# A pair's two state stores joined into one, and one gather tile in 128 fetched row by row by SyncE

## The chip, the cores and the metric

The kernel runs on one core of a Trainium2 chip. The metric is device time in microseconds. A core has TensorE (PE) for matrix products, VectorE (DVE), ScalarE (ACT) and GpSimd (POOL), each with its own instruction queue, and SyncE (SP), which here does nothing but issue transfers and wait. SyncE and GpSimd both issue transfers (DMAs), and these run on the same 16 DMA engines.

## The reference

A graph layer: 12500 nodes of 128 features, 400000 edges sorted by destination, 8 heads of 16 channels (C).

```python
h   = relu(layernorm(x))
hn  = layernorm(h) * ln1_g + ln1_b
x_l, x_r = hn @ W_l, hn @ W_r                       # per node
# every edge, and one self loop a node with the mean edge_attr
m     = leaky_relu(x_l[src] + x_r[dst] + edge_attr @ W_e, 0.2)
alpha = sum over channels of m * att                # one score per edge and head
a     = softmax of alpha over the edges of each dst
out   = segment_sum(x_l[src] * a, dst) + bias
h     = h + out
y     = x + h + gelu(layernorm(h) @ W1 + b1) @ W2 + b2
```

So every edge needs the x_l row of its source, which is anywhere in memory, and every destination needs a softmax and a sum over some 32 neighbouring edges.

## The kernel before

**Units and pairs.** The sorted edges are cut into units of 256 (U). Two units make a pair (UP), of four tiles of 128 edges; there are 3125 tiles and 782 pairs. A unit holds about 8 destinations, and the kernel gives it a window of 16 nodes (NW): for each of these 16 x 8 node-heads it collects the lowest score, the sum of weights and the weighted sum of rows, 18 numbers (SH, 72 bytes) in each of 128 partitions. This record is stored to memory at the window's place, and the final stage reads the records back by node. Since windows of neighbouring units overlap, there are two state tensors: even units write to the first, odd ones to the second. A later window of the same tensor may overwrite only what the earlier one did not use, so the stores to one tensor must land in order; their addresses come from registers, and each store waits until the one before it to its tensor has landed. A test on the device, `fits`, checks from the destinations that all windows hold their units; if not, a slower general path runs.

**Before the main loop** the node features are normalised tile by tile (`node_stages`, rounds of four tiles), the x_l rows (136 numbers, 544 bytes) are stored to `xl_dram`, and the destinations are turned into differences (`from_first`, `as_float`, `differ`) and into the addresses of windows (`edge_constants`, L369 and L370). GpSimd meanwhile gathers raw rows of x for 29 pairs ("raw" pairs): their x_l is computed later from them, so they need no gather in the main loop.

**The main loop** is written out by hand: rounds r from -4 on, and in each round every stage runs for the pair that is due (`stages`, L1538 to L1562). The order of that text is the order of each engine's queue. Pair c is gathered in round c-4 (`gather`, L955, GpSimd, one indirect transfer a tile, with 128 row numbers each), placed by DVE at the end of round c-1 (`place`, L995), multiplied on TensorE in round c (`combine`, L1009 and L1012), then scored, weighed, and collected in round c+6 (`collect`, L1072). In round c+7 DVE takes each node's own heads (`own_heads`, L1081 and L1087) and SyncE stores the record (`put`, L1098). A pair's gathered rows `xs` stand in one of 12 buffers, which is free again after `collect`.

**SyncE's queue in a round**, in order: rows of a raw pair if one is due (L950); in every second of the first 196 rounds 512 KB of edge attributes for their mean (`sum_load`, L1107); in every eighth round up to 104 two stores that clear a part of the state (`clear`, L728); loads and stores of the final stage (L1151 to L1159, L1401) and of the row tables (L632 to L719); in every fourth round the four loads of the next four pairs (`windows`, three rounds ahead: ea, dl, du, then a register load L938 and zw); last the two stores of `put`, with a register load of eight addresses in every fourth round. SyncE stops at the first instruction whose condition is not met, and all behind it waits.

```python
stages = ((-AHEAD, gather), (LATE + 1, own_heads), (5, keep_turned), (0, combine), ...
          (3, weigh), (-1, place))
late_stages = ((-WAHEAD, windows), (LATE + 1, put))
AHEAD, LATE, WAHEAD, QP = 4, 6, 3, 4
rows = es.enter_context(tc.tile_pool(name="e_rows", bufs=AHEAD + LATE + 2))
```

Of the kernel before, what the change touches and what calls it, by code (L numbers as in the profile page):

```python
# [13 lines left out]
F32 = mybir.dt.float32  # L14
# [8 lines left out]
P = 128  # L23
# [21 lines left out]
PW = OR * OS  # L45
CW = UP * NW
WN = P - DE
# [15 lines left out]
LEAD = 2  # L63
KEPT = 7
BIG = 2.0**126
CAP = 2.0**120
# [77 lines left out]
def tile_gnn(  # L144
# [55 lines left out]
    first_sb = keep.tile([1, NU], I32, name="first_sb")  # L200
    win_sb = keep.tile([1, NU // QU], I32, name="win_sb")
    flag = keep.tile([1, 1], I32, name="flag")
    quads = [(t, min(GN, NT - t)) for t in range(0, NT, GN)]
# [47 lines left out]
    def load_consts():  # L251
# [9 lines left out]
        nc.sync.dma_start(b2_r, row_bcast(b2, P))  # L261
        nc.sync.dma_start(first_sb, bass.AP(tensor=dst.tensor, offset=dst.offset, ap=[[0, 1], [U, NU]]))
# [102 lines left out]
    def edge_constants():  # L365
        of = build.tile([P, H], F32, name="of")
        mine = build.tile([P, H], F32, name="mine")
        below = build.tile([P, P // NW], F32, name="below")
        nc.vector.tensor_scalar(win_sb, first_sb[:, 0:NU:QU], float(P * 4), None, op0=OP.mult)  # L369
        nc.vector.tensor_scalar(first_sb, first_sb, float(H * SH * 4), None, op0=OP.mult)  # L370
        nc.vector.tensor_copy(
# [28 lines left out]
    bad = rng.tile([RP, PARTS + 1], F32, name="bad")  # L400
    junk = rng.tile([RP, EP], BF16, name="junk")
    nf = rng.tile([RP, RU], F32, name="nf")
    dlb = rng.tile([RP, EP], BF16, name="dlb")
    dlr = rng.tile([RP, RU // UP, OR, OS], BF16, name="dlr")
# [10 lines left out]
    def from_first():  # L415
        nc.vector.tensor_copy(nf, dc[:, 0:EP:U])
        nc.vector.memset(dlr[:, :, :, OW:OS], 0.0)
        nc.vector.tensor_scalar(nf, nf, -1.0, None, op0=OP.mult)

# [11 lines left out]
    def differ(i):  # L431
        for u in range(UP * i, UP * i + UP):
            es = slice(u * U, (u + 1) * U)
            nc.scalar.activation(dlb[:, es], df[:, es], AF.Identity, bias=nf[:, u : u + 1])
        e = UP * U * i
        nc.scalar.activation(
            dlr[:, i, :, 0:OW], df[:, e : e + OR * OW].rearrange("p (a b) -> p a b", b=OW), AF.Identity,
            bias=nf[:, i // QP * QU : i // QP * QU + 1],
        )
# [7 lines left out]
    def fits():  # L447

        fu = rng.tile([RP, RU + 2], F32, name="fu")
        lf = rng.tile([RP, RU], F32, name="lf")  # L450
        real = rng.tile([RP, RU], F32, name="real")
        off = rng.tile([RP, 4, RU], F32, name="off")
# [3 lines left out]
        nc.vector.tensor_copy(fu, df[:, 0 : (RU + 1) * U + 1 : U])  # L456
        nc.vector.tensor_copy(lf, lu)

        nc.vector.tensor_sub(off[:, 0], lf, fu[:, 0:RU])
        nc.vector.tensor_sub(  # L460
# [3 lines left out]
        )  # L464
        nc.vector.tensor_tensor(off[:, 2], lf, fu[:, 2 : RU + 2], op=OP.is_ge)
        nc.vector.tensor_scalar(real, lf, float(NO_NODE // 2), None, op0=OP.is_lt)
# [9 lines left out]
        nc.vector.tensor_scalar(off[:, 3], place, float(SPARE**2), None, op0=OP.is_gt)  # L476
        nc.vector.tensor_mul(off, off, real[:, None, :].to_broadcast([RP, 4, RU]))
        nc.vector.tensor_reduce(bad[:, PARTS : PARTS + 1], off.rearrange("p k u -> p (k u)"), AX.X, OP.max)
# [272 lines left out]
    with tc.manual_schedule():  # L751
# [15 lines left out]
        for r in range(max(max(len(qs), 9) + LAST + 1, 16 + PARTS, rows_at[-1] + KEPT + 1)):  # L767
# [11 lines left out]
            if r == 14:  # L779
                nc.sync.dma_start(src_sb, src)  # L780
            if r == 10:
                from_first()
# [26 lines left out]
    with tc.If(fast == 1) as cmp:  # L809
        window_edges(  # L810
            tc, n_edges, ea_t, NT, NE, NUE, ident, wer, weh, negrep, diag, nid, farw, bias_r, b2_r, w1_sb, w2_sb,
            cols, xl_dram, xl_t, xr_dram, xr_t, dc_dram, du_dram, late_dram, state, clear, xr_steps, qs, raw_steps, raw, x_t, out_t, h_sb, src_sb, first_sb, win_sb, wid,
        )
# [67 lines left out]
def window_edges(  # L881
    tc, n_edges, ea_t, NT, NE, NUE, ident, wer, weh, negrep, diag, nid, farw, bias_r, b2_r, w1_sb, w2_sb,
    cols, xl_dram, xl_t, xr_dram, xr_t, dc_dram, du_dram, late_dram, state, clear, xr_steps, qs, raw_steps, raw, x_t, out_t, h_sb, src_sb, first_sb, win_sb, wid,
):
# [27 lines left out]
    with ExitStack() as es:  # L912
# [30 lines left out]
        def rows_at(t, at, n, size):  # L943

            return t.rearrange("n f -> (n f)").bitcast(U8)[ds(at, n * size)].rearrange("(n f) -> n f", f=size)

        def gather(c):
            xs = rows.tile([P, KP, XW], F32, name="xs")
# [4 lines left out]
            for t in tiles_of(c):  # L953
                for j in t:
                    nc.gpsimd.indirect_dma_start(  # L955
                        out=xs[:, j, :],
# [47 lines left out]
        def combine(c):  # L1004
# [3 lines left out]
            for j in range(e // P):  # L1008
                nc.tensor.matmul(  # L1009
                    z[:, j * P : (j + 1) * P], d["xs"][:, j, 0:P], ident, start=(j == 0), stop=False, is_transpose=True  # L1010
                )
# [53 lines left out]
        def collect(c):  # L1065
# [4 lines left out]
            for i, js in enumerate(tiles_of(c)):  # L1070
                for j in js:
                    nc.tensor.matmul(  # L1072
                        d["acc"][:, i, :], d["pt"][:, j * P : (j + 1) * P], d["xs"][:, j, :],
                        start=(j == js[0]), stop=(j == js[-1]),
                    )
# [15 lines left out]
        def put(c):  # L1091
            if c % QP == 0:
                at = words(first_sb[0:1, UP * c : UP * (c + QP)], (NT * P - CW) * H * SH * 4)
                for i in range(c, min(c + QP, n_pr)):
                    pairs[i]["put"] = at[UP * (i - c) : UP * (i - c + 1)]
            for i in range(len(tiles_of(c))):
                u = UP * c + i
                nc.sync.dma_start(  # L1098
                    rows_at(state[u % 2], pairs[c]["put"][i], NW * H, SH * 4), pairs[c]["rec"][:, i, :].bitcast(U8)
                )  # L1100

# [814 lines left out]
```

## Time and profile before

| | |
|---|---|
| median of three runs | 3963.11 us (3962.49 to 3964.65) |
| the profiled execution | 3958.53 us, span 3956.7 us |
| mean granted TensorE clock | 0.943 |
| PE busy | 3459.6 us (87%), 18462 instructions |
| POOL busy | 2957.3 us (75%), 3138 instructions |
| DVE busy | 2794.0 us (71%) |
| ACT busy | 2172.3 us (55%) |
| SyncE's transfers | 490760 packets, 330.85 MB, 35.7% of 16 DMA engines |
| GpSimd's transfers | 100000 packets, 217.32 MB, 31.1% |

How to read it: L12 is a line of the kernel. A group's row names line, engine, operation, output<-input and count, then the busy time and the mean of one in ns, then the engine's idle time just before and what ended it. In the rows of one line the three numbers are the shortest, median and longest duration in ns, followed by when the first and the last one start. A wait's row gives who waited, for whom, microseconds in total, how often, and the longest. In a timeline a row is start, length, engine, line and count; several instructions may be merged into one row. A window's row gives its stretch, its length, the busy time of PE, PE's weight loads, DVE, ACT and POOL with their counts, the granted clock, the share of time in which the DMA engines were busy, and GB/s. "q" behind an engine means its queue: SyncE shows only in this form.

### The profile page before, as it was taken

The page shows a single profiled execution, that of the slowest core. Times are in us where ns is not written, and L with a number is a line of the kernel's source. Part 1 is how long each engine was busy: PE and PEld are TensorE (multiplying, and loading weights), DVE is VectorE, ACT ScalarE, POOL GpSimd, SP SyncE. Part 2 cuts the span into 40 slices and gives each one's busy share as a digit, 9 for nine tenths or more (in the row PEclk, how much of TensorE's full clock was granted, in tenths as well). Part 3 has the DMA queues.
Part 4 walks back from the last instruction along what each step waited for, and adds up shares of the span by engine and source line. Part 5 has one row for each costly group of instructions (what it writes and reads, how often), then busy time and mean ns, then how long its engine had stood idle before and what let it go on. Part 6 is the DMA issues. An engine that isn't in the chain of part 4 may idle for free.

```text
span 3956.7 us, 60318 instructions
## 1 busy us (share of the span) xinstructions
PE 3459.6 (87%) x18462; PEld 2360.4 (60%) x18463; DVE 2794.0 (71%) x6131; ACT 2172.3 (55%) x4747; POOL 2957.3 (75%) x3138
## 2 busy tenths in 40 slices
PE   4589888898898899989889899898998998999888
PEld 3356565666566566666666666666665665666565
DVE  6477777877777777677767776677767666667665
ACT  7445555555565555555555555555555455455454
POOL 7777777777777777777777777777777777777774
PEclk6799999999999999999999999999999999999999
DMA  8788888777766666666666666666666665666663
GB/s 227 206 189 196 191 198 193 176 178 174 164 127 125 127 122 123 127 122 117 118 123 129 122 122 128 122 123 122 114 124 129 125 123 108 119 123 113 120 119 75
DMA packets 591812, 552.26 MB, mean 140 GB/s; under 512 B 299169, under 2 KB 469762, under 8 KB 591058
## 3 DMA queue, kind: packets, MB, share of 16 engines
q1 hardware_dynamic: 490760, 330.85, 35.7%
q0 software_dynamic: 100000, 217.32, 31.1%
q8 instruction: 150, 2.46, 0.3%
q14 instruction: 182, 1.49, 0.1%
q10 hardware_dynamic: 720, 0.13, 0.0%
HBM read 482.05 MB, written 65.88 MB: 138 GB/s over the span
## 4 chain that ended last, share of the span: by engine, by line
PE 40%; DMA 24%; POOL 20%; issue 11%; ACT 2%; DVE 2%; SPq 1%; POOLq 0%; DVEq 0%
DMA xs<-xl_dram,src_sb 22%; POOL xs L955 19%; PE z L1012 9%; PE acc L1072 9%; PE ab L1033 7%; PE pt_ps L1058 5%; PE z L1009 4%; PE ab L1018 2%; PE acc L1356 1%; PE acc L1381 1%; ACT h_sb L532 1%; SPq L308 1%; ACT sq L557 0%; DVE rec L1039 0%; PE pt_ps L700 0%
## 5 line engine op out<-in xcount | busy, mean ns | idle before, releaser
L955 POOL DMA_INDIRECT xs<-xl_dram,src_sb x3009 | 2842.2, 945 | 917.0 <-issue 794.8
L1050 ACT ACTIVATE p<-ab,rec 128x256 f32<-128x256 f32 x1563 | 656.3, 471 | 982.8 <-DVE rec L1039 974.2
L1081 DVE TENSOR_TENSOR own<-acc,diag 128x272 f32<-128x272 f32 x782 | 341.9, 437 | 845.3 <-PE acc L1072 837.4
L1009 PE MATMUL z<-ident,xs 128*128 128x128 f32 x3125 | 562.2, 283 | 383.1 <-DMA xs<-xl_dram,src_sb 343.5
L1072 PE MATMUL acc<-xs,pt 128*128 128x136 f32 x6250 | 892.1, 288 | 0.0
L1012 PE MATMUL z<-ea,zw 128*128 128x512 f32 x1564 | 854.4, 630 | 17.2 <-DMA zw<-xr_dram 10.8
L1009 PEld LDWEIGHTS z<-ident,xs 128*128 128x128 f32 x3125 | 398.9, 142 | 785.1 <-DMA xs<-xl_dram,src_sb 438.4
L1072 PEld LDWEIGHTS acc<-xs,pt 128*128 128x128 f32 x6250 | 821.3, 199 | 0.0
L1033 PE MATMUL ab<-m,negrep 128*128 128x512 f32 x1564 | 805.0, 596 | 0.0
L1063 ACT COPY pt<-pt_ps 128x512 f32<-128x512 f32 x782 | 455.6, 583 | 614.2 <-PE pt_ps L1058 606.0
L1058 PEld LDWEIGHTS pt_ps<-ident,p 128*128 128x128 f32 x3125 | 416.9, 149 | 361.3 <-issue 288.8
L1028 DVE TENSOR_TENSOR m<-z,zs 128x512 f32<-128x512 f32 x782 | 532.8, 681 | 128.0 <-ACT zs L1023 126.9
L995 DVE TENSOR_SCALAR ea<-dl,wid 96x516 f32<-96x516 bf16 x782 | 575.6, 736 | 24.3 <-DMA dl<-dc_dram 24.3
L1039 DVE TENSOR_REDUCE rec<-ab 128x2 f32<-128x512 f32 x781 | 538.4, 689 | 12.3 <-PE ab L1033 11.7
L1058 PE MATMUL pt_ps<-ident,p 128*128 128x128 f32 x3125 | 500.6, 286 | 1.7 <-ACT pt L1063 1.0
L1023 ACT ACTIVATE zs<-z 128x512 f32<-128x512 f32 x782 | 472.2, 604 | 43.9 <-DMA xs<-xl_dram,src_sb 37.5
L1087 DVE TENSOR_REDUCE rec<-own 128x34 f32<-128x272 f32 x782 | 340.8, 436 | 26.7
L1018 PE MATMUL ab<-ne,farw 128*128 128x512 bf16 x782 | 314.2, 402 | 20.0 <-ACT p L1050 18.8
L1012 PEld LDWEIGHTS z<-ea,zw 128*128 128x128 f32 x1564 | 257.6, 206 | 20.2 <-DVE ne L1002 10.8
L1033 PEld LDWEIGHTS ab<-m,negrep 128*128 128x128 f32 x1564 | 245.7, 195 | 1.1 <-DMA ea_s<-in_ea_t 0.7
L1018 PEld LDWEIGHTS <-farw 128*128 128x128 bf16 x782 | 79.6, 102 | 215.5 <-issue 110.5
L1050 ACT ACT_TABLE_LOAD x104 | 133.4, 1283 | 1.8
(232 smaller groups left out, 2168.3 us busy)
## 6 DMA issues: line engine op xcount, KB each, us to landing
dl<-dc_dram SPq DMA_DIRECT2D x196, 396.0 KB
ea<-in_ea_t SPq DMA_DIRECT2D x196, 256.0 KB
ea_s<-in_ea_t SPq DMA_DIRECT2D x98, 512.0 KB
xs<-xl_dram,src_sb POOLq DMA_INDIRECT x3009
state<-rec SPq DMA_DIRECT2D x1563, 9.0 KB
state<-empty SPq DMA_DIRECT2D x28, 504.0 KB
f_st<-state SPq DMA_DIRECT2D x46, 288.0 KB
du<-du_dram SPq DMA_DIRECT2D x196, 64.0 KB
```

The costliest lines, as they stand in the source:

```text
L955: nc.gpsimd.indirect_dma_start(out=xs[:, j, :], out_offset=None, in_=xl_dram, in_offset=bass.IndirectOffsetOnAxis(ap=src_sb[:, c * KP + j ...
L995: nc.vector.tensor_scalar(d["ea"][0:WN].rearrange("p (a b) -> p a b", b=OW), d["dl"][0:WN].rearrange("p (a b) -> p a b", b=OS)[:, :, 0:OW] ...
L1009: nc.tensor.matmul(z[:, j * P : (j + 1) * P], d["xs"][:, j, 0:P], ident, start=(j == 0), stop=False, is_transpose=True)
L1012: nc.tensor.matmul(z[:, :e], d["zw"], d["ea"][:, :e], start=False, stop=True)
L1018: nc.tensor.matmul(d["ab"][:, :e], d["far"], d["ne"][:, :e], start=True, stop=False)
L1023: nc.scalar.activation(d["zs"][:, :e], d["z"][:, :e], AF.Copy, scale=SLOPE)
L1028: nc.vector.tensor_tensor(d["m"][:, :e], d["z"][:, :e], d["zs"][:, :e], op=OP.max)
L1033: nc.tensor.matmul(d["ab"][:, :e], negrep.rearrange("p n h -> p (n h)"), d["m"][:, :e], start=False, stop=True)
L1039: nc.vector.tensor_reduce(d["rec"][:, :, CX], d["ab"].rearrange("p (u e) -> p u e", e=U), AX.X, OP.min)
L1050: nc.scalar.activation(d["p"][:, us], d["ab"][:, us], AF.Exp, bias=d["rec"][:, i, CX:SH], scale=-1.0)
L1058: nc.tensor.transpose(d["pt_ps"][:, js], d["p"][:, js], ident)
L1072: nc.tensor.matmul(d["acc"][:, i, :], d["pt"][:, j * P : (j + 1) * P], d["xs"][:, j, :], start=(j == js[0]), stop=(j == js[-1]),)
```

## The change

**One store for a pair.** The two states become slices of one tensor `state_dram`, with a spacing such that the windows of both units of a pair lie at a fixed distance. A pair now has one base, the smaller of (first destination of unit 0) + 12 and (first destination of unit 1). Unit 0's window starts at base - 12 (BEFORE), unit 1's at base - 3 (AFTER). One transfer with an address pattern of 128 partitions x 2 units x 72 bytes stores both records; `put` reads four addresses instead of eight in every fourth round. The starts used for the differences and for the test of windows are those of the new windows, computed on DVE before the main loop; the test has one more condition.

**Rows fetched by SyncE.** For some pairs (`hand_pairs`) GpSimd doesn't gather the last tile. Starting in round 8, and again every 32 rounds, SyncE fetches the 128 x_l rows of one such tile one by one, four (HR) in each of 32 rounds, into a tile of its own (two buffers), at the very beginning of the round. The pair is used 33 rounds after its first row (one more if it would be a raw pair). The row addresses are prepared before the main loop: 24 small loads of row numbers, one a handed tile, in round 14 behind the load of all row numbers, and one DVE multiply by the row's size in round 16. In the main loop SyncE reads 16 addresses into registers in every fourth round. `combine` and `collect` take these rows from the new tile (`row_of`).

```diff
+HR = 4
+HAND_AT = 8
+HAND_LEAD = 1
+def hand_pairs(nt, n_edges):
+    late = {c for c, _ in raw_pairs(nt, n_edges)}
+    n_full = n_edges // (UP * U)
+    hands, r = [], HAND_AT
+    while True:
+        c = r + P // HR + HAND_LEAD
+        while c in late:
+            c += 1
+        if c >= n_full:
+            return hands
+        hands.append({"c": c, "i": len(hands), "round": r})
+        r += P // HR
...
-    state = [dram.tile([NT * P * H, SH], F32, name=f"state{i}") for i in range(2)]
+    SR = (BEFORE + NT * P + NW) * H
+    state_dram = dram.tile([NT * P * H + 2 * (SR + (BEFORE - AFTER) * H), SH], F32, name="state")
+    state = [state_dram[i * SR + BEFORE * H : i * SR + (BEFORE + NT * P) * H] for i in range(2)]
...
-        nc.vector.tensor_scalar(first_sb, first_sb, float(H * SH * 4), None, op0=OP.mult)
+        nc.vector.tensor_scalar(first_sb, first_sb, float(BEFORE), None, op0=OP.add)
+        nc.vector.tensor_tensor(base_sb, base_sb, first_sb, op=OP.min)
+        nc.vector.tensor_scalar(base_sb, base_sb, float(H * SH * 4), None, op0=OP.mult)
...
             if r == 14:
                 nc.sync.dma_start(src_sb, src)
+                for d in hands:
+                    at = src.offset + (d["c"] + 1) * UP * KU - 1
+                    nc.sync.dma_start(
+                        hand_sb[d["i"] : d["i"] + 1, :],
+                        bass.AP(tensor=src.tensor, offset=at, ap=[[0, 1], [NCH * K, P]]),
+                    )
+            if r == 16:
+                nc.vector.tensor_scalar(hand_sb, hand_sb, float(XW * 4), None, op0=OP.mult)
...
+        def hand(r):
+            for d in hands:
+                k = r - d["round"]
+                if not 0 <= k < P // HR:
+                    continue
+                if k == 0:
+                    d["x"] = once.tile([P, XW], F32, name=f"hand{d['i'] % 2}")
+                if k % QP == 0:
+                    d["at"] = words(hand_sb[d["i"] : d["i"] + 1, k * HR : (k + QP) * HR], (NT * P - 1) * XW * 4)
+                for i in range(k * HR, (k + 1) * HR):
+                    nc.sync.dma_start(d["x"][i : i + 1, :].bitcast(U8), rows_at(xl_dram, d["at"][i - k // QP * QP * HR], 1, XW * 4))
...
             for t in tiles_of(c):
                 for j in t:
+                    if c in of_hand and j == KP - 1:
+                        continue
                     nc.gpsimd.indirect_dma_start(
...
         def put(c):
             if c % QP == 0:
-                at = words(first_sb[0:1, UP * c : UP * (c + QP)], (NT * P - CW) * H * SH * 4)
+                at = words(base_sb[0:1, c : c + QP], NT * P * H * SH * 4)
                 for i in range(c, min(c + QP, n_pr)):
-                    pairs[i]["put"] = at[UP * (i - c) : UP * (i - c + 1)]
-            for i in range(len(tiles_of(c))):
-                u = UP * c + i
-                nc.sync.dma_start(
-                    rows_at(state[u % 2], pairs[c]["put"][i], NW * H, SH * 4), pairs[c]["rec"][:, i, :].bitcast(U8)
-                )
+                    pairs[i]["put"] = at[i - c]
+            d, nu = pairs[c], len(tiles_of(c))
+            nc.sync.dma_start(states_at(d["put"])[:, 0:nu], d["rec"][:, 0:nu].bitcast(U8))
...
             for r in range(-AHEAD, max(last_round, groups[-1]["round"] + 18)):
                 in_round(r, early, groups[:-2])
+                hand(r)
```

More of the change, by code (lines that the diff above doesn't have):

```diff
@@ L455, in fits @@
         nc.vector.memset(ones, 1.0)
[L456 removed]
         nc.vector.tensor_copy(lf, lu)
[L459 removed]
+        nc.vector.tensor_sub(off[:, 0], lf, start[:, 0:RU])
         nc.vector.tensor_sub(
@@ L882, in window_edges @@
     tc, n_edges, ea_t, NT, NE, NUE, ident, wer, weh, negrep, diag, nid, farw, bias_r, b2_r, w1_sb, w2_sb,
-    cols, xl_dram, xl_t, xr_dram, xr_t, dc_dram, du_dram, late_dram, state, clear, xr_steps, qs, raw_steps, raw, x_t, out_t, h_sb, src_sb, first_sb, win_sb, wid,
+    cols, xl_dram, xl_t, xr_dram, xr_t, dc_dram, du_dram, late_dram, state_dram, state, clear, xr_steps, qs, raw_steps, raw, x_t, out_t, h_sb, src_sb, base_sb, win_sb, hand_sb, hands, wid,
 ):
```

53 lines of the change are left out of this document (39 added, 14 removed).

## The prediction

> **What bounds the kernel now.** I read the page's groups and chain first, then GpSimd's gather line, then SyncE's waits cut into three stretches, because the change takes work from GpSimd and gives it to SyncE.
>
> ```profile
> DMA xs<-xl_dram,src_sb 22%; POOL xs L955 19%; PE z L1012 9%; PE acc L1072 9%; PE ab L1033 7%; PE pt_ps L1058 5%; PE z L1009 4%; PE ab L1018 2%; PE acc L1356 1%; PE acc L1381 1%; ACT h_sb L532 1%; SPq L308 1%; ACT sq L557 0%; DVE rec L1039 0%; PE pt_ps L700 0%
> L955 POOL DMA_INDIRECT xs<-xl_dram,src_sb x3009 | 2842.2, 945 | 917.0 <-issue 794.8
> ...
> L955 POOL DMA_INDIRECT xs<-xl_dram,src_sb x3009: 940/944/1242, 152.9 to 3910.9; - x189
> L1012 PE MATMUL z<-ea,zw x1564: 275/595/1192, 167.0 to 3917.0; 128*128 128x512 f32 x196
> ```
>
> 3009 gathers start between 152.9 and 3910.9 us: (3910.9 - 152.9) / 3008 = 1.249 us each, 945 ns busy and 0.30 us of issue, with nothing in between. GpSimd never waits, so it paces the kernel from end to end, and TensorE's last z stands only 6 us behind the last gather. A gather less is worth 1.249 us, as long as nothing makes GpSimd wait.
>
> Now SyncE. The three windows are: the rounds in which the state is still being cleared, the rest of the edge-sum loads, and the remainder.
>
> ```profile
> 195.00:695.00 500.00, 437.76 (x2300) 295.24 (x2299) 372.36 (x719) 261.30 (x570) 377.78 (x402) 0.95 0.82 193
> 695.00:1090.00 395.00, 351.94 (x1889) 238.83 (x1888) 310.67 (x614) 221.00 (x486) 298.69 (x317) 0.96 0.75 173
> 1090.00:3900.00 2810.00, 2533.47 (x13654) 1726.15 (x13653) 1965.58 (x4141) 1542.10 (x3151) 2124.60 (x2250) 0.96 0.63 122
> ```
> ```profile
> SPq L1098 <- DMA state<-rec: 141.1, 79, 5.6
> SPq L1098 <- DMA state<-empty: 77.5, 26, 6.8
> SPq L728 <- DMA state<-rec: 19.1, 21, 2.6
> SPq L1098 <- DVE rec L1087: 14.2, 11, 2.6
> ...
> SPq L1098 <- DMA state<-rec: 116.8, 67, 5.1
> SPq L1098 <- DVE rec L1087: 78.1, 46, 5.3
> ...
> SPq L1098 <- DMA state<-rec: 740.8, 376, 6.6
> SPq L1098 <- DVE rec L1087: 635.3, 319, 5.9
> ```
> ```profile
> L1098 SPq DMA_DIRECT2D state<-rec x204: 332/344/1893, 200.9 to 691.3; - x102
> ...
> L1098 SPq DMA_DIRECT2D state<-rec x174: 332/337/1164, 695.8 to 1089.4; - x174
> ...
> L1098 SPq DMA_DIRECT2D state<-rec x1160: 332/337/1408, 1094.6 to 3896.9; - x194
> ...
> L995 DVE TENSOR_SCALAR ea<-dl,wid x103: 734/736/747, 199.1 to 691.7; 96x516 f32<-96x516 bf16 x103
> ...
>   DMA dl<-dc_dram: 17.2, 4
> ```
>
> The first four wait rows are those of 195 to 695 us, the next two those of 695 to 1090, the last two those of 1090 to 3900; then come the state's stores in each stretch, two a round, so 102, 87 and 580 rounds. In the first stretch a round takes some 4.85 us (103 placements in 500 us), the DMA engines are busy for 0.82 of the time (last but one column), and SyncE waits for DVE, that is for work to become ready, only 14.2 us. It is the state's stores and clears that it waits for: it is late. DVE already waits 17.2 us there for the window loads that SyncE issues. From 1090 us on it waits 635 us for DVE: there it has time to spare. So SyncE is the second resource near its limit, and only early.
>
> **The change part by part.**
>
> Gathers removed: tiles are handed to SyncE from rounds 8, 40, ... 744, which makes 24 (a pair that would be raw is stepped over; the target of round 744 is pair 777, inside the 781 full pairs). 24 x 1.249 = 30.0 us off GpSimd, which goes to 2985 gathers.
>
> Row fetches added to SyncE: 24 x 128 = 3072 one-row transfers, four in each of rounds 8 to 775. Nearest rows are the loads of dst into single partitions (L323 and L332), and what follows each at its heels:
>
> ```profile
> 24.59 3.45 SPq L319 DMA_DIRECT2D dc<-in_dst  x2
> 28.15 0.22 SPq L323 DMA_DIRECT2D dc<-in_dst  x1
> 28.42 0.32 SPq L328 DMA_DIRECT2D dc<-in_dst  x1
> 28.78 0.27 SPq L332 DMA_DIRECT2D dc<-in_dst  x1
> 29.10 0.36 SPq L254 DMA_DIRECT2D cols<-in_ln_g  x1
> 29.50 0.43 SPq L254 DMA_DIRECT2D cols<-in_ln_b  x1
> 32.80 8.06 SPq L254 DMA_DIRECT2D cols<-in_b  x2
> ...
> SPq L254 <- DMA dc<-in_dst: 7.4, 1, 7.4
> ...
> L1098 SPq MOVE state<-rec x1563: 29/29/38, 183.3 to 3932.5; - x196
> L938 SPq TENSOR_LOAD <-win_sb x196: 514/749/924, 159.6 to 3900.3; - x196
> L938 SPq TENSOR_LOAD <-first_sb x196: 524/535/563, 182.6 to 3929.9; - x196
> ```
>
> 0.22 to 0.34 us of issue, plus a MOVE of 0.03 for the address, plus some 0.1 of steps between instructions (28.15 + 0.22 to 28.42 is 0.05, twice): 0.31 to 0.47 us a row. I take 0.36, as a single partition issues nearer to 0.22: 4 x 0.36 = 1.44 us a round. Sixteen addresses are read every fourth round, by one load (0.54 to 0.75) or two: 0.13 to 0.38 a round; I take 0.17. Eight loads of dst partitions went out without one waiting for another, so rows of one tile need not wait for each other either.
>
> The joined store takes one issue of 0.34 (the median of the stores' rows) and 0.03 with its step off every round, -0.41 us; its 256 pieces of 72 bytes are the same as before in two transfers, and it still waits for the store before it. Net SyncE work: 1.44 + 0.17 - 0.41 = 1.20 us a round.
>
> In the last stretch this has cover: (741 + 635) / 580 rounds = 2.4 us of waiting a round. In the first it doesn't. 102 rounds x 1.20 = 122 us. What can take it in: waits for DVE, 22 us (14.2 and the small rows of the same kind); the clears' waits for a store, 19 us, since the rows stand ahead of them; and the 79 waits of a store for the store before it, of which rows can fill at most 79 x 1.44 = 114. The rows are one lump per round while these waits go up to 5.6, so I take half, 60. The 77.5 us behind a clear they can't fill: rows come ahead of the clear in the round, the store behind it.
>
> A new wait: the second cols<-in_b (40.5, inside the 8.06 of the row) waits 7.4 us for a load of dst that it shares nothing with, and it is the eighth issue after that load. So SyncE has eight completion counters in turn, and an issue waits for the landing of the one eight before it. In 195 to 695 us it issues:
>
> ```profile
> ea_s<-in_ea_t SPq DMA_DIRECT2D x51, 512.0 KB
> state<-empty SPq DMA_DIRECT2D x25, 504.0 KB
> dl<-dc_dram SPq DMA_DIRECT2D x26, 396.0 KB
> ea<-in_ea_t SPq DMA_DIRECT2D x26, 256.0 KB
> ...
> state<-rec SPq DMA_DIRECT2D x204, 9.0 KB
> du<-du_dram SPq DMA_DIRECT2D x26, 64.0 KB
> ```
>
> With zw (26) and 21 of the row tables, 405, or 4.0 a round: a counter comes round after 9.8 us. After the change it is 4.0 - 1 + 4 = 7.0 a round: 5.6 us. A 9 KB store behind a window load was waited for up to 5.6 us, one behind a clear up to 6.8; there are ten such large transfers in eight rounds. Bounds 0 and 100 us in the stretch (10 x 0.8 us per eight rounds); I take 50.
>
> Sum: SyncE falls behind by 122 - 22 - 19 - 60 + 50 = 71 us by 695 us (bounds 0 and 200). Who waits: the window loads queue behind the rows, DVE places with them, TensorE needs DVE's output, and all three fall back at once, since dl already lands just in time. GpSimd runs on until it needs the buffer of twelve pairs ago, which is free when that pair is collected, six rounds after its z. It is some two rounds ahead now (6 us at the end, more with the landing), so four rounds or 19 us of lag cost nothing, and the other 52 us stop GpSimd. Lost there they don't come back, although SyncE and TensorE catch up later (TensorE is busy 2533 of 2810 us).
>
> By the Trainium skill, page "DMA: Bandwidth & Descriptors", section "Anatomy of one DMA — SWDGE (gpsimd) path", a DMA takes about 2.0 us and its bytes over 436 GB/s, so that even 512 KB lands in 3.2 us. No counter would then be waited for in a lap of 5.6 us, the 50 us would be 0, the lag 21, and the time that of the first rival. The waits of up to 5.6 us for 9 KB stores say that with the engines at 0.82 it takes longer here.
>
> Before the main loop, 24 loads of row addresses go out behind the 1.5 MB of src, and a DVE multiply waits for all of them:
>
> ```profile
> 70.92 0.61 SPq L780 DMA_DIRECT2D src_sb<-in_src  x1
> ...
> 135.39 0.52 SPq L586 DMA_DIRECT2D xl_dram<-xl  x1
> ...
> 152.92 0.94 POOL L955 DMA_INDIRECT xs<-xl_dram,src_sb  x1 [0.30 <-issue]
> ```
>
> 24 issues at 0.4 are 10 us, with three laps of counters perhaps 15; the last x_l store at 135.4 is needed by the first gather at 152.9, 17 us later less its landing. Mostly covered: 0 to 6 us, I take 2. The few small DVE operations added hide in the same gap.
>
> Total: -30 + 52 + 2 = +24 us. The profiled execution took 3958.5 us (span 3956.7), 4.6 below the median of 3963.1; I add to the median: 3987.
>
> **The rivals.** (A) The rows fit into SyncE's waits. For it: 238 us of landing waits in the early stretch, twice what is added. If all 114 are filled and no counter is waited for, the lag is below the free 19 us, and the time is 3963 - 30 + 2 = 3935. It decides at a lag of 49 us: below, the kernel gains.
> (B) SyncE stays behind until the edge-sum loads end at 1090 us (one 512 KB load every second round, DMA at 0.75): there waits for DVE and stores are (78 + 117) / 87 = 2.2 us a round, against it. With rows at 0.45 and two address loads the net is 1.8 a round and GpSimd loses about 130: 4063.
> (C) The gain and the loss cancel: lag of 41 to 57 us, 3955 to 3971.
> (D) The change does something else. If rows of one tile waited for each other, four landings a round would make the kernel milliseconds longer; the dst loads speak against it. If the new range test failed, the general path would run; I worked the test out on the drawn destinations, and the largest distance from a window's start is 13 of 15 allowed.
>
> **How the numbers follow.** Under 0.2% (8 us) a measurement of this kernel could not be told from no change. Forecast, slower by 8 to 72 us: 0.47. A: 0.34. B and beyond: 0.11. C: 0.07. D: 0.01. So faster 0.34, same 0.07, slower 0.59. The range must take in A on one side, from 3930, and the forecast on the other, to 4035; the forecast's own range is 3971 to 4035.
>
> **What would show it.** 2985 gathers at the same 945 ns; SyncE's waits for DVE near zero before 700 us and large after 1100; DVE waiting for dl well over 17 us; GpSimd with waits for TensorE's acc (buffers) between 300 and 700 us, some 50 us in all, and none later. The forecast is wrong if GpSimd still takes a gather every 1.25 us in the first 700 us (then A), or if it waits beyond 1100 us (then B).

## The result

The changed kernel takes 3981.1 us (median of six runs, 3971.8 to 3984.2), the kernel before 3963.0 (six runs, 3962.3 to 3964.7): a ratio of 1.0044, 95% interval 1.0033 to 1.0055, slower by 18 us. The profiled execution, whose trace is read below, is the longest of the six: 3984.2 us (span 3982.4), 25.6 us more than the one of before. The prediction was 24 us on the median. Each ratio below is to the kernel before timed beside that run, which takes 3957 to 3963 us, but 4708 to 4765 us beside seven of the runs.

### The profile after

From the page: shares of the chain by line, and the group of the gathers. Then the rows of the gather's line, and GpSimd's waits at that line between 195 and 760 us (us in total, times).

```profile
POOL xs L1028 18%; DMA xs<-xl_dram,src_sb 16%; PE z L1085 8%; PE acc L1145 7%; PE ab L1106 6%; PE pt_ps L1131 4%; PE z L1082 4%; PE ab L1091 2%; DMA dl<-dc_dram 2%; DMA ea_s<-in_ea_t 2%; DMA state<-rec 1%; DMA state<-empty 1%; DMA du<-du_dram 1%; SPq L1012 1%; DMA zw<-xr_dram 1%
L1028 POOL DMA_INDIRECT xs<-xl_dram,src_sb x2985 | 2822.6, 946 | 960.0 <-issue 782.5
```
```profile
L1028 POOL DMA_INDIRECT xs<-xl_dram,src_sb x2985: 940/945/1226, 156.7 to 3935.0; - x199
...
  issue: 106.1, 348
  PE acc L1145: 51.0, 13
```

The chain now runs through things that were not in it: SyncE's rows (L1012), the state's stores and clears, the window loads. Between 390 and 745 us no gather is among its largest parts, and the clears of the state lead it; in the same stretch before, the gathers and their landings made 35% of it:

```profile
by line: DMA state<-empty 12.1%; issue 8.5%; PE z L1085 7.1%; PE acc L1145 6.5%; DMA dl<-dc_dram 6.4%; DMA state<-rec 6.0%; DMA du<-du_dram 5.8%; PE ab L1106 5.6%; SPq L1012 5.2%; DMA late_dram<-l_xl 4.5%; PE pt_ps L1131 3.4%; SPq L983 3.2%
```

The gathers can be added up. At the old pace, 3758.0 us over 3008 steps or 1.2493 us, 2985 gathers take 2984 x 1.2493 = 3728.0 us. They took 3935.0 - 156.7 = 3778.3. So GpSimd lost 50.3 us on the way, it started 3.8 us later than before (152.9), and 24 gathers less saved 30.0: +24.1 us at the last gather. Of the 50.3, 47 are the nine waits for acc of 0.8 to 11.6 us (the 51.0 us above less the 0.3 that each of the 13 would have anyway); the other 3 are gathers that took 1 ns longer each.

Where it stood still: two of the nine places, in GpSimd's timeline (start, length, and in brackets the idle time before it and what ended it). All nine lie between 395 and 740 us, some 43 us apart, which is the distance of the clears, eight rounds.

```profile
487.53 0.94 POOL L1028 DMA_INDIRECT xs<-xl_dram,src_sb  x1 [8.31 <-PE acc L1145]
488.78 0.94 POOL L1028 DMA_INDIRECT xs<-xl_dram,src_sb  x1 [0.30 <-issue]
...
532.55 0.94 POOL L1028 DMA_INDIRECT xs<-xl_dram,src_sb  x1 [11.60 <-PE acc L1145]
```

SyncE's waits from 195 to 695 us, 94 rounds now (who waited, for what, us in total, times, longest):

```profile
SPq L1170 <- DMA state<-empty: 78.0, 12, 7.9
SPq L1170 <- DMA state<-rec: 47.6, 41, 2.5
SPq L1170 <- DVE rec L1160: 15.9, 4, 14.4
SPq L1177 <- DMA dl<-dc_dram: 15.6, 16, 1.6
SPq L1052 <- DMA ea_s<-in_ea_t: 6.5, 6, 1.6
SPq L1052 <- DMA late_dram<-l_xl: 6.0, 5, 1.6
SPq L1047 <- DMA ea_s<-in_ea_t: 3.6, 5, 1.0
SPq L1012 <- DMA ea<-in_ea_t: 3.5, 4, 1.7
...
SPq L765 <- DMA state<-rec: 0.5, 1, 0.5
```

The store's waits for the store before it fell from 141.1 to 47.6 us, the clear's from 19.1 to 0.5: the rows went into them. The 78 us behind the clears stayed. New are the waits of a transfer for one that it shares nothing with: the load of edge attributes (L1177) waits for dl, the row fetch (L1012) for ea. With the small ones they make 37 us. These are the eight counters of the prediction: in the trace every issue of SyncE carries the counter of the eighth issue before it, from the thirteenth on.

By the Trainium skill, page "DMA: Bandwidth & Descriptors", section "Anatomy of one DMA — SWDGE (gpsimd) path", about 2.0 us and the bytes over 436 GB/s, dl's 396 KB would have landed 2.9 us after their issue (an estimate from that page, whose fit is of transfers that GpSimd issues, while dl is SyncE's). The trace differs: in the 16 waits above, dl landed 4.9 to 7.6 us after its issue.

It is not that the rows fill the DMA engines. From 195 to 695 us these are busy for 0.74 of the time, less than the 0.82 of before, and move 176 GB/s instead of 193 (the last two numbers of the row):

```profile
195.00:695.00 500.00, 402.70 (x2092) 271.26 (x2091) 342.58 (x666) 238.71 (x528) 349.77 (x371) 0.90 0.74 176
```

Nor do the rows come late for their own pair: TensorE waits for them 7.6 us, 6 times, in the whole run.

What SyncE's own instructions cost, and DVE's wait before the main loop:

```profile
L1012 SPq MOVE hand<-xl_dram x3072: 29/29/38, 201.9 to 3910.1; - x192
L1012 SPq DMA_DIRECT2D hand<-xl_dram x3072: 224/228/405, 202.0 to 3910.2; - x192
...
L983 SPq TENSOR_LOAD <-hand_sb x192: 977/1012/1152, 200.9 to 3892.9; - x192
...
L1170 SPq DMA_DIRECT2D state<-rec x782: 350/417/1338, 200.4 to 3958.4; - x196
```
```profile
DVE hand_sb L825 <- DMA hand_sb<-in_src: 17.9, 1, 17.9
```

### The profile page after: what moved, and what is told of

Same layout as the page of the kernel before. It is cut to its first block, busy times and chain, and to the rows that moved or that the text cites. A ratio compares the mean times of both kernels' runs of the same rounds, so it can differ in the third digit from the quotient of the medians.

```text
span 3982.4 us, 64960 instructions
## 1 busy us (share of the span) xinstructions
PE 3447.6 (87%) x18462; PEld 2354.5 (59%) x18463; DVE 2800.3 (70%) x6138; ACT 2165.7 (54%) x4747; POOL 2937.5 (74%) x3114
## 4 chain that ended last, share of the span: by engine, by line
PE 33%; DMA 26%; POOL 18%; issue 12%; DVE 4%; SPq 3%; ACT 1%; POOLq 0%; DVEq 0%
POOL xs L1028 18%; DMA xs<-xl_dram,src_sb 16%; PE z L1085 8%; PE acc L1145 7%; PE ab L1106 6%; PE pt_ps L1131 4%; PE z L1082 4%; PE ab L1091 2%; DMA dl<-dc_dram 2%; DMA ea_s<-in_ea_t 2%; DMA state<-rec 1%; DMA state<-empty 1%; DMA du<-du_dram 1%; SPq L1012 1%; DMA zw<-xr_dram 1%
## 5 line engine op out<-in xcount | busy, mean ns | idle before, releaser
L1082 PE MATMUL z<-ident,xs 128*128 128x128 f32 x3101 | 553.0, 283 | 343.1 <-DMA xs<-xl_dram,src_sb 266.1
L1145 PEld LDWEIGHTS acc<-xs,pt 128*128 128x128 f32 x6202 | 812.9, 198 | 0.0
L1183 DVE TENSOR_REDUCE part<-ea_s 128x1 f32<-128x1024 f32 x98 | 118.8, 1212 | 37.2 <-DMA ea_s<-in_ea_t 37.0
```

Source lines behind the costliest of these rows:

```text
L1082: nc.tensor.matmul(z[:, j * P : (j + 1) * P], row_of(c, j)[:, 0:P], ident, start=(j == 0), stop=False, is_transpose=True)
L1145: nc.tensor.matmul(d["acc"][:, i, :], d["pt"][:, j * P : (j + 1) * P], row_of(c, j), start=(j == js[0]), stop=(j == js[-1]),)
```

## The experiments

Theory 1 is that of the prediction: SyncE is short of time only while it clears the state and loads edge sums; rows make it late there, the window loads come late, and GpSimd runs out of buffers; later rows are free. Theory 2: the joined store costs, not the rows. Theory 3: every handed tile costs about 2 us, wherever it runs, and saves 1.25.

Five runs stand in the table beside the changed kernel, since their gathers can be added up in the same way. "Lost" is last minus first gather less 1.2493 us a step; up to 1.5 us of it can be gathers that are a fraction of a ns slower, 3 us in the changed kernel.

| | ratio to before, interval | gathers | first to last gather | lost |
|---|---|---|---|---|
| changed kernel | 1.0044 (1.0033 to 1.0055) | 2985 | 156.7 to 3935.0 | 50.3 |
| joined store alone | 1.0006 (0.9997 to 1.0016) | 3009 | 153.2 to 3912.5 | 1.4 |
| rows from round 112 | 0.9943 (0.9926 to 0.9959) | 2989 | 154.3 to 3887.6 | 0.4 |
| rows ahead of the store | 1.0023 (1.0013 to 1.0033) | 2985 | 155.7 to 3914.9 | 31.2 |
| two stores, rows | 1.0174 (1.0157 to 1.0191) | 2985 | 156.3 to 3976.2 | 91.9 |
| 32, then 24 rounds a tile | 0.9942 (0.9926 to 0.9959) | 2983 | 162.6 to 3888.6 | 0.6 |

### The joined store alone

```diff
-    hands = hand_pairs(NT, n_edges)
+    hands = []
```

> The joined store alone: no tile is handed over, GpSimd gathers all 3009 tiles. Theory 1 (SyncE is late only while it clears the state and loads edge sums, in the first 700 us, and the rows push it over the edge there; the joined store takes some 0.4 us a round off it): GpSimd takes a gather every 1.249 us as before and never waits, so 3959 to 3966 us, the same as before; SyncE's waits for the state's previous store grow by what the issue saves. Theory 2 (the rows cost little; what stops GpSimd in the changed kernel is the joined store, which waits for one landing of both units where two stores waited for two landings in parallel): the 51 us of GpSimd's waits stay although there are no rows, so some 4010 us. Theory 3 (every handed tile costs about as much as it saves, wherever it runs): the same as before, as in theory 1.

3960.6 us against 3958.6 of the kernel before on the same chip: no difference that can be measured. GpSimd's longest wait for TensorE's acc is the 0.3 us that every gather has, and SyncE waits longer for the previous store, where it had waited for two:

```profile
POOL xs L1026 <- PE acc L1143: 14.3, 47, 0.3
```
```profile
SPq L1168 <- DMA state<-rec: 185.6, 72, 5.4
SPq L1168 <- DMA state<-empty: 76.6, 14, 7.6
```

Theory 2 falls: all of the loss needs the rows.

### Rows from round 112

```diff
-HAND_AT = 8
+HAND_AT = 112
```

> Rows as in the changed kernel, but the first tile starts in round 112 instead of 8, behind the last clear (round 104): 20 handed tiles instead of 24. Theory 1: no wait of GpSimd in 195 to 740 us; 20 x 1.249 = 25.0 us saved, 3 of them lost before the main loop: 3941 us (3936 to 3952, since edge sums are still loaded until round 196). Theory 2 (the joined store): the waits of 51 us between 400 and 740 us stay: 3986. Theory 3 (each handed tile costs 18 + 30 = 48 us over 24, that is 2.0 us, wherever it runs): 3963 + 20 x 0.75 = 3978.

3935.7 against 3958.6 us, 22.9 faster. By the table, 20 gathers less are 25.0, of which the later start takes 1.4 and the way 0.4: 23.2. GpSimd waits nowhere for a buffer, although a round has four rows, as in the changed kernel, while edge sums are still being loaded:

```profile
POOL xs L1028 <- PE acc L1145: 21.6, 71, 0.3
```

Theory 3 falls, and theory 1 stands in its main point: 20 of the 24 tiles earn all that they save, and the whole loss needs the rows of rounds 8 to 111. Later rows are not free for SyncE: against the kernel before, its dl loads fall back by 11 us between pairs 108 and 144, with edge sums still to load. That much GpSimd doesn't feel.

### Rows ahead of the store

```diff
                 in_round(r, early, groups[:-2])
-                hand(r)
...
                 for late, f in late_stages:
                     c = r - late
+                    if f is put:
+                        hand(r)
```

> The changed kernel with the four rows of a round issued just ahead of the state's store, behind clear and window loads, instead of at the head of the round. Theory 1 (what counts is SyncE's sum of issue and waits in the first 110 rounds): in a round with a clear (12 of them) the rows now fill the wait of up to 7.9 us for the clear to land, 1.3 us each, 16 us less lag, so that GpSimd's waits come down from 51 to about 35 us: 3965 (3958 to 3972). Counter theory (waits for completion counters are a large part): the rows now stand right behind the 400 KB window loads, the counters are waited for at least as much as before: 3981 or more.

GpSimd lost 31 us instead of 50, and the kernel is 8 us slower than before instead of 18: within theory 1's range (5 faster to 9 slower than the 3963 it starts from), at its upper end. SyncE's waits from 195 to 695 us show why, and that the other theory has a part:

```profile
SPq L1177 <- DMA dl<-dc_dram: 20.6, 18, 2.4
SPq L765 <- DMA state<-rec: 20.5, 12, 2.2
SPq L1170 <- DMA state<-empty: 20.4, 11, 3.6
...
SPq L1170 <- DMA ea<-in_ea_t: 16.5, 19, 1.8
SPq L1012 <- DMA ea_s<-in_ea_t: 15.8, 19, 2.2
```

The wait behind the clears fell from 78.0 to 20.4 us. Of these 58 us, 20 came back at once as the clear's own wait for the store, and more as waits for ea, ea_s, dl and the like, which the rows and the store now meet: with the small ones these went from 37 to 73 us. GpSimd got back 19 us, so moving work into a wait paid a third of the wait.

### Two stores again, with the rows

```diff
-    state_dram = dram.tile([NT * P * H + 2 * (SR + (BEFORE - AFTER) * H), SH], F32, name="state")
+    state_dram = [dram.tile([SR, SH], F32, name=f"state{i}") for i in range(2)]
...
-            nc.sync.dma_start(states_at(d["put"])[:, 0:nu], d["rec"][:, 0:nu].bitcast(U8))
+            for i in range(nu):
+                nc.sync.dma_start(
+                    rows_at(state_dram[i], d["put"], NW * H, SH * 4), d["rec"][:, i, :].bitcast(U8)
+                )
```

> The changed kernel with two stores a pair again, one to a state tensor each, at the same register address; rows and everything else as changed. Theory 1: SyncE has some 0.35 to 0.4 us more to issue in a round, for the 110 rounds in which it is late, of which part lies in waits that it has anyway: 20 to 45 us more of GpSimd's waits, 4001 to 4026. Theory 2 (the joined store is what costs): GpSimd's waits are gone, 3936. Theory 3 (each tile costs wherever it is): 3981, as the changed kernel.

4025.7 us against 3958.6, 67 slower, 4 us beyond theory 1's range (38 to 63 above the 3963 it starts from). GpSimd lost 91.9 us, 42 more than in the changed kernel, which is within the 20 to 45 expected. Its waits over the whole span, then those after 765 us:

```profile
POOL xs L1020 <- PE acc L1137: 115.2, 79, 11.9
...
POOL xs L1020 <- PE acc L1137: 27.4, 15, 5.1
```

Of the second row some 23 us are more than the usual 0.3 a gather; the last such wait ends at 1229 us, while the changed kernel has none after 740. So with one store more SyncE stays late enough to stop GpSimd until the edge sums have been loaded, and not only while the state is cleared.

With rows, then, a store less in a round is worth 42 us, and without rows nothing (the first experiment). A saving on SyncE has a price only where SyncE is the late one. The second store brings an issue, a landing to wait for and a counter at once; the run doesn't separate these.

### More tiles, and the addresses in two transfers

```diff
+MORE_AT = 208
-HAND_AT = 8
+HAND_AT = 112
...
+        n = P // HR if r < MORE_AT else 24
+        c = r + n + HAND_LEAD
...
-                for d in hands:
-                    at = src.offset + (d["c"] + 1) * UP * KU - 1
-                    nc.sync.dma_start(
-                        hand_sb[d["i"] : d["i"] + 1, :],
-                        bass.AP(tensor=src.tensor, offset=at, ap=[[0, 1], [NCH * K, P]]),
-                    )
+                for n in (P // HR, 24):
+                    ds = [d for d in hands if d["n"] == n]
+                    at = [src.offset + (d["c"] + 1) * UP * KU - 1 for d in ds]
...
+                    nc.sync.dma_start(
+                        hand_sb[ds[0]["i"] : ds[-1]["i"] + 1, :],
+                        bass.AP(tensor=src.tensor, offset=at[0], ap=[[at[1] - at[0], len(at)], [NCH * K, P]]),
+                    )
...
+                a, b = (P * i // d["n"] for i in (k, k + 1))
```

> Rows from round 112 on, three tiles over 32 rounds each as long as edge sums are loaded, then 23 over 24 rounds each: 26 tiles, their addresses read by two transfers. Theory 1, on a chip where GpSimd gathers every 1.249 us without pauses: 26 x 1.249 = 32.5 us saved, 0 to 2 lost before the main loop, and SyncE, which with four rows a round has some 1.2 us a round of waits left after 1090 us, takes 0.45 us more in them without GpSimd waiting: a ratio of 0.9915 to 0.9925, below the 0.9943 of 20 tiles. If those waits can't be filled by rows, GpSimd's waits show after 1090 us and the ratio is 0.995 or more. Where GpSimd pauses on its own and a row takes 0.63 us of SyncE (as on two chips above), SyncE is late throughout and the ratio is about 1.013.

3935.2 against 3957.3 us: as fast as with 20 tiles, not faster. The first half of the expectation held. With five or six rows a round after round 208 GpSimd waits for no buffer, and SyncE still waits for DVE's rec, 95 us in 1090 to 2500 and 144 in 2500 to 3900. The second half failed: six gathers more are worth 7.5 us, but the first gather starts at 162.6 us instead of 154.3. Two transfers of 3 and 23 rows of single words land later than 20 small ones, and DVE stands at the multiply for them:

```profile
DVE hand_sb L829 <- DMA hand_sb<-in_src: 23.9, 1, 23.9
```
```profile
L824 SPq DMA_DIRECT2D hand_sb<-in_src x2: 638/3474/6310, 73.3 to 73.9; - x2
L829 DVE TENSOR_SCALAR hand_sb<-hand_sb x1: 215/215/215, 102.3 to 102.3; 26x128 int32<-26x128 int32 x1
```

DVE's wait and the start of the gathers go together over three kernels: 15.9 us and +1.4 (20 loads), 17.9 and +3.8 (24 loads), 23.9 and +9.7 (two transfers). From the first to the last, 8.0 us more of waiting move the start by 8.3. What follows on DVE's queue is the normalisation of x, from which the x_l rows are made; the wait comes out at the start of the gathers in part only: in all three some 14 us of it are covered.

### Seven runs that don't answer

In these seven GpSimd pauses about every 11.8 us, with rows or without (timelines below), so a difference in them can't be put down to the edit alone. Six were made before the run with 26 tiles, whose expectation speaks of them, and one after it.

SyncE's time without transfers: the joined store alone, with two register loads a round that nothing reads.

```diff
         def hand(r):
+            if HAND_AT <= r < HAND_AT + 768:
+                words(base_sb[0:1, 0:16], NT * P * H * SH * 4)
+                words(base_sb[0:1, 16:17], NT * P * H * SH * 4)
```

> The joined store alone, and in each of the 768 rounds in which the changed kernel fetches rows SyncE loads 16 words and one word into registers that nothing reads: no row transfer, no handed tile, 3009 gathers, but about the same time of SyncE, 0.98 + 0.55 us a round against 4 x 0.325 + 0.25. If SyncE's issue time alone is what counts: GpSimd's waits stay at some 47 us, all 24 tiles' gain is missing, 3963 + 47 = 4010 by the scale of the median before, a ratio of 1.012. If the waits for completion counters (37 us in 195 to 695 us) add to it, they are gone here: 10 to 25 us of GpSimd's waits, a ratio of 1.003 to 1.006. If the transfers' traffic is the cost: 1.000.

1.0046 (1.0031 to 1.0061).

Only the first three tiles:

```diff
-        if c >= n_full:
+        if c >= n_full or r > 104:
```

> The changed kernel with only its first three handed tiles, whose rows are fetched in rounds 8 to 103; from round 104 SyncE has no row to fetch. Theory 1: nearly all of the loss is made in these rounds: 3 x 1.249 = 3.7 us saved, GpSimd's waits up to 653 us (35 us) and perhaps part of those after it (12), so 31 to 43 us above the kernel before and 13 to 25 us above the changed kernel with its 24 tiles, a ratio of 1.008 to 1.011. Rival (each handed tile costs 2.0 us wherever it runs): 3 x 0.75 = 2 us above the kernel before, a ratio of 1.0006.

1.0072 (1.0048 to 1.0096), 39 us.

Rows by ScalarE, twice:

```diff
-                row, engines=[SP], min_val=0, max_val=top,
+                row, engines=[engine], min_val=0, max_val=top,
...
-                    nc.sync.dma_start(d["x"][i : i + 1, :].bitcast(U8), rows_at(xl_dram, d["at"][i - k // QP * QP * HR], 1, XW * 4))
+                    nc.scalar.dma_start(d["x"][i : i + 1, :].bitcast(U8), rows_at(xl_dram, d["at"][i - k // QP * QP * HR], 1, XW * 4))
```

> The changed kernel with the same row transfers, and the loads of their addresses, issued by ScalarE instead of SyncE: the same bytes, places and rounds. Theory 1 (it is SyncE's own time that is short early): SyncE is as with the joined store alone, GpSimd's waits of 47 us between 390 and 740 us go, and all 24 tiles pay: 30 us below the kernel before, less 3 before the main loop, so a ratio of 0.993; ScalarE takes 1.6 us more a round and has room (55% busy). Rival (the transfers themselves are the cost, by what they do to the DMA engines or by the landings that others then wait for): GpSimd's waits stay at 30 us or more, a ratio of 1.001 or above.

> The rows by ScalarE once more, for the same reason. Theory 1 (SyncE's own time is short early): GpSimd's waits in 390 to 740 us are gone, ratio 0.993, if ScalarE can carry the rows. On the chip of the run before ScalarE waited 510 us for landings of rows ahead of its work (completion counters of its own issues); if that happens here too, ScalarE is late with the turned weights in every round, and the ratio is above 1.000 with GpSimd's waits spread over the whole span instead of ending at 740 us. If the transfers themselves cost, whoever issues them: GpSimd's waits as in the changed kernel, 47 us, all before 740 us.

1.0149 (1.0125 to 1.0173) and 1.0158 (1.0141 to 1.0175). In the first of the two ScalarE stands 431.3 us, 186 times, ahead of its copy of the turned weights (`pt`) until rows have landed, and 368.2 us in the second; how much of that is due to the pauses isn't known.

27 tiles over 24 rounds each from round 112, twice:

```diff
+HROUNDS = 24
-HAND_AT = 8
+HAND_AT = 112
...
-        c = r + P // HR + HAND_LEAD
+        c = r + HROUNDS + HAND_LEAD
```

> A version by theory 1: the first tile in round 112, a tile's rows spread over 24 rounds instead of 32 (five or six a round), 27 tiles, and all their addresses read by one transfer instead of 24. Theory 1: 27 x 1.249 = 33.7 us saved, none lost before the main loop; SyncE's 1.15 us of waits a round that are left after 1090 us must take 0.5 us more, between 695 and 1090 us they hardly do: 0 to 8 us of GpSimd's waits there. A ratio of 0.9915 to 0.9935. Rival (each tile costs 2.0 us and saves 1.249): above 1.000.

> The 27 tiles over 24 rounds each from round 112 with one transfer for the addresses, once more, since on the chip of the four runs before GpSimd itself paused 1.6 us or more every nine gathers or so, rows or none, and the kernel before took 4708 us. Where GpSimd takes a gather every 1.249 us without a pause, theory 1 stands as it was: 33.7 us saved, 0 to 8 lost between 695 and 1090 us or later, a ratio of 0.9915 to 0.9935; better than the 0.9943 of 20 tiles. If SyncE with 5.33 rows a round has no time left after 1090 us (as on that chip, where it waited 8 us for DVE in 1400 to 3900 us), GpSimd waits there too and the ratio is 0.995 or above.

1.0130 (1.0109 to 1.0150) and 1.0144 (1.0117 to 1.0172).

26 tiles with one small address load in each round before the main loop, and the multiply at its end:

```diff
+            if 15 <= r < 15 + len(hands):
+                d = hands[r - 15]
+                at = src.offset + (d["c"] + 1) * UP * KU - 1
+                nc.sync.dma_start(
+                    hand_sb[d["i"] : d["i"] + 1, :],
+                    bass.AP(tensor=src.tensor, offset=at, ap=[[0, 1], [NCH * K, P]]),
+                )
-            if r == 16:
-                nc.vector.tensor_scalar(hand_sb, hand_sb, float(XW * 4), None, op0=OP.mult)
...
+        nc.vector.tensor_scalar(hand_sb, hand_sb, float(XW * 4), None, op0=OP.mult)
         clear(0)
```

> The kernel of the run before (26 tiles, 32 and then 24 rounds each), with the row addresses read by 26 loads again, one in each round before the main loop, and the multiply at the end of that part instead of round 16. In the run before the first gather started at 162.6 us against 152.9 before the change, since DVE stood at the multiply for 23.9 us (17.9 us in the changed kernel, with 24 loads in a row). If that wait is what moves the start, the first gather starts at 153 to 154.5 us and the ratio falls from 0.9942 to about 0.992 (3926 to 3929 us where the kernel before takes 3957 to 3959). If SyncE's time for 26 loads is what moves it, the first gather stays at 156 us or later: 0.9925 or more.

1.0135 (1.0112 to 1.0158).

The numbers of the register loads and of the first three tiles lie in or near what theory 1 expected, those of the 27 tiles don't, and neither counts, for the pauses. In the last run the first gather starts at 194.4 us, where the other six start at 188.6 to 202.9, so its question isn't answered either. With the register loads, GpSimd's and DVE's timelines round 1485 us:

```profile
1482.38 0.94 POOL L1029 DMA_INDIRECT xs<-xl_dram,src_sb  x1 [0.30 <-issue]
1485.24 0.94 POOL L1029 DMA_INDIRECT xs<-xl_dram,src_sb  x1 [1.92 <-remote]
...
1494.01 0.95 POOL L1029 DMA_INDIRECT xs<-xl_dram,src_sb  x1 [0.30 <-issue]
1496.93 0.94 POOL L1029 DMA_INDIRECT xs<-xl_dram,src_sb  x1 [1.97 <-PE ab L1107]
```
```profile
1485.01 0.44 DVE L1155 TENSOR_TENSOR own<-acc,diag 128x272 f32<-128x272 f32 x1 [5.14 <-PE pt_ps L1132]
...
1496.69 0.44 DVE L1155 TENSOR_TENSOR own<-acc,diag 128x272 f32<-128x272 f32 x1 [5.18 <-PE ab L1107]
```

Left open are therefore three questions: how much of the loss is SyncE's issue time and how much the waits for counters, whether ScalarE could carry the rows, and whether 26 tiles with spread address loads reach the 3927 us or so that the table's sum would give (3935.2 less the 8 or 9 us of the late start).

## Why the prediction was right

It held in sign and in its mechanism: SyncE falls behind while the state is cleared, the window loads come late, and GpSimd runs out of buffers. That the size came so close is in part luck, since errors in the lag and in the free lag cancel. Against its steps:

**Pace.** 2985 gathers at 945 ns, a step of 1.249 us wherever GpSimd doesn't wait. Right; 24 gathers saved 30.0 us.

**SyncE's sum per round.** Net +1.20 forecast. A row takes 0.33 us (1.33 us for the four in the timeline at 202 us) where 0.36 was taken: 1.31. The 16 addresses come in one load, but of 1.01 us, not 0.54 to 0.75: 0.25 instead of 0.17. The joined store issues in 0.417 us, not in the 0.34 of one of the two, so it saves 0.33, not 0.41. Sum 1.23: three errors that cancel.

**What the waits take in.** The changed kernel's waits cover 94 rounds, those of before 102, so per round and for 102 rounds: waits for the previous store 141.1 to 51.6, that is 89 us filled (60 forecast, 114 the bound); the clear's wait 18.6 filled (19 forecast); the waits for DVE some 9 (22 forecast; 14.4 of the 15.9 us are one wait at the first store, which in the kernel before ended at 192.9 us, outside the window); counter waits 41 new (50 forecast); and the waits behind the clears, which the forecast left as they were, 7 longer (77.5 to 84.6). The lag by these rows is 102 x 1.23 - 89 - 19 - 9 + 41 + 7 = 56 us. The starts of the dl loads agree: they fall back by 51 us between the first pair and pair 108 and by 62 until pair 144, at 890 us, against 71 forecast for 695 us. The largest mis-sized term is the filling of the store's waits, half of the bound where three quarters were filled.

**From lag to standing still.** 19 us of free lag were forecast, and 52 us of waits of GpSimd. The first stop comes at 395 us, when the dl loads have fallen back by 18 us, and the stops add up to 47. Right in kind, but 56 us less 19 would be 37. The free lag is not 19 throughout. It can be read in the kernel before as the time from `own_heads` of a pair, which follows its `collect`, to the first gather of the pair twelve later, whose buffer this frees. For the gather of pair 50 that is 16 us; for that of pair 114, the last one at which the changed kernel stops, 6.6 us. Before, then after, `own_heads` of pair 102 and the first gather of pair 114:

```profile
685.81 0.44 DVE L1081 TENSOR_TENSOR own<-acc,diag 128x272 f32<-128x272 f32 x1 [1.59 <-PE acc L1072]
692.36 0.94 POOL L955 DMA_INDIRECT xs<-xl_dram,src_sb  x1 [0.30 <-issue]
...
739.69 0.44 DVE L1154 TENSOR_TENSOR own<-acc,diag 128x272 f32<-128x272 f32 x1 [1.01 <-PE acc L1145]
739.92 0.95 POOL L1028 DMA_INDIRECT xs<-xl_dram,src_sb  x1 [3.06 <-PE acc L1145]
```

`own_heads` is 53.9 us later there, and 53.9 - 6.6 = 47.3 is, within 0.3 us, what the gather is late by (47.6). So a lag forecast 15 us too large and a free lag forecast up to 12 us too large made 52 where 47 was measured.

**Where.** "None later" than 700 us is nearly right: the last stop ends at 740. But SyncE was not free from 695 us on; its lag grew until 890 us, and the waits for DVE are back only after 1090, with 335.9 us. GpSimd's stops end with the clears (round 104), not with SyncE's lateness. DVE waited for dl as forecast: 46.7 us in 195 to 695, 17.2 before.

**Start.** 2 us taken, 0 to 6 allowed, 3.8 measured. The step names the multiply's wait, but prices SyncE's issue (0.4 us a load, where the median is 0.60) and the last x_l store; what sets it is DVE, which stands 17.9 us at the multiply.

**The rivals.** (A), all rows into the waits, came closer than its working: 89 of the 114 us were filled. By the sum above it failed on the counter waits: the lag without them is 56 - 41 = 15 us, below its 19, though not below the 6.6 read here; no run shows this. (B), late until 1090 us, is right about SyncE and wrong about GpSimd; with two stores a pair again GpSimd's stops last as long, though they cost 92 us and not 130. The limits of (C), and the 49 us at which (A) is said to turn, leave out the 2 us of the start. The median is 6 us below the forecast; the runs of the changed kernel spread over 12 us and those of before over 2, so the stops probably differ in length from run to run, which only one trace of each can't show.

## What to carry to other kernels

A queue's waits over the whole span don't say where it has room for work; cut them by stage, and charge added work to the stage in which the queue waits for landings, not for data. Rows from round 112 on were worth 23 us, and with four tiles more, from round 8 on, they were a loss of 18, so ask of a spread-out change when each part of it runs before judging it whole. Work moved to the queue that another engine's loads go through can come back as that engine's lack of buffers, here in the rhythm of the queue's largest items.

## What was not expected of the hardware

The load of 16 words into registers took SyncE 1.01 us, and one of four words 0.56: not proportional, and as long as three row fetches. A transfer for one 544-byte row takes 0.228 us to issue, one with 256 pieces of 72 bytes 0.417. Two transfers of 384 and 2944 single words had landed 29.0 us after the first was issued (73.3 to the multiply at 102.3), 20 loads of 128 words each after 21.2 us, so that reading single words in one large strided transfer gained nothing.

In seven of the runs GpSimd's gathers paused for some 1.8 us more than usual about every 11.8 us (medians), and in the timelines above DVE resumes with it. The steps of SyncE from one row to the next (those under 2 us, from 1400 to 3900 us) took 0.63 us on average with 27 tiles there, against 0.40 in the changed kernel. One of the chips showed no such pauses in another run (26 tiles, two address transfers). What sets them isn't shown.
